# Adding a norm's shifts by a one-row product in the PSUM bank, in place of an add on VectorE

## The chip, the cores and the metric

The kernel runs on one core of a Trainium2 chip. The metric is the device time of one execution in microseconds (us); "before" is the median of three runs. Five engines work side by side and meet at semaphores: TensorE (PE in the profile, its weight loads PEld), VectorE (DVE), ScalarE (ACT), GpSimd (POOL) and the queue engine SyncE (SP), which issues DMAs.

## The reference

Two transformer-like layers are applied to x of shape 4 x 2048 x 256, in f32. Each layer derives six rows of 256 values per batch from a condition (shift, scale and gate, twice), and uses them around two blocks:

```python
mod = (_silu(L1_c) @ L1_wmod).reshape(L1_c.shape[0], 6, 1, -1)
sa, ca, ga, sb, cb, gb = (mod[:, 0], mod[:, 1], mod[:, 2], mod[:, 3], mod[:, 4], mod[:, 5])
...
h = _layernorm(x, axis=-1) * (1 + ca) + sa
x = x + ga * _L1_attn_ref(h, L1_attn_A_log, L1_attn_B, L1_attn_C, L1_attn_D)
h = _layernorm(x, axis=-1) * (1 + cb) + sb
x = x + gb * _L1_ffn_ref(h, L1_ffn_W_r, L1_ffn_W_k, L1_ffn_W_v, L1_ffn_mu_r, L1_ffn_mu_k)
```

Layer 0 is a linear attention and a mixture of 48 experts. Layer 1 is a state-space filter along the sequence (a long convolution per channel) and a gated feed-forward net. The change concerns the first norm of layer 1, `_layernorm(x) * (1 + ca) + sa`, which feeds the filter.

## The kernel before

The four stages run one after the other: `attention`, `experts`, `ssm` and `mix`. The stage `ssm` begins with the norm. The sequence of 8192 tokens (4 batches of 2048) is cut into 16 blocks of 512 tokens; a block is a tile of 128 partitions x 4 x 256 channels (`NT` = 4, `NB` = 4 blocks for each batch).

For each block n the norm does this:

- `see(n)`: the block is loaded by a DMA on SyncE's queue (L1260; the first waits until the experts' last scatters into `acc` have landed), and VectorE takes the statistics of its four parts (L1267 and L1268).
- `affine(mv, name, eng)` (L178): mean and variance become a bias and a scale per token. Inside it `rsqrt` (L155) makes four preparing operations on VectorE and three Newton steps of four operations each (L171 to L174). Without `eng` the Newton steps run on GpSimd. Blocks 0 and 1 have a call each, named n4, with `nc.vector`; from block 2 on one call, named n8, serves a pair of blocks and runs on GpSimd.
- `normal(n)`: ScalarE writes the normalized block `xh`, one activation for each part (L1274).
- `turn(n)`: VectorE multiplies `xh` by the scales `cb` (L1280) and adds the shifts `sb` (L1281). Both rows are held on all 128 partitions, loaded by a broadcasting DMA (`row`, L138). Then TensorE multiplies by a constant matrix that reverses the order of the 128 tokens (L1285), two products of 128 x 128 by 128 x 512 into two PSUM banks.
- `evict(n)`: ScalarE copies the two banks into `hch`, with channels ahead of tokens (L1292).

There are four banks (`pn`, bufs=4), so two blocks can be in them, and three tiles `xh`. The order on VectorE and ScalarE is pinned to the order of the program (`in_order`): in the loop over pairs, ScalarE normalizes blocks n-2 and n-1, then copies block n-3 out; VectorE takes the statistics of blocks n and n+1 and their bias and scale, then turns n-2 and n-1; ScalarE copies n-2 out between. The order on TensorE is chosen by the scheduler.

After the norm, the filter works on groups of 32 channels: products with the taps (L1374, 128 contraction rows), block states (L1360), and products with the carried states (L1380, 16 contraction rows). They use `hch` of all blocks, so they begin when the norm is done. The last stage, `mix`, calls `affine` with `nc.vector` for its block 0 and on GpSimd for the others.

Of the kernel before, what the change touches and what calls it, by code (L numbers as in the profile page):

```python
# [9 lines left out]
F32 = mybir.dt.float32  # L10
# [4 lines left out]
ALU = mybir.AluOpType  # L15
# [4 lines left out]
P = 128  # L20
B, N, D = 4, 2048, 256
# [4 lines left out]
NT = 4  # L26
# [19 lines left out]
class Net:  # L46
# [105 lines left out]
        nc.vector.scalar_tensor_tensor(out, sign, 1.0, mag, ALU.subtract, ALU.mult)  # L152


    def rsqrt(self, mv, name, eng=None):  # L155

        nc = self.nc
        n = mv.shape[1]
        eng = eng or nc.gpsimd

        def col(t):
            return self.stat.tile([P, n], F32, name=f"{name}{t}")

        v, nh, y = col("v"), col("h"), col("y")
        nc.vector.tensor_scalar(v, mv[:, :, 1], EPS_LN, None, ALU.add)
        nc.vector.tensor_scalar(nh, v, -0.5, None, ALU.mult)
        nc.vector.tensor_scalar(y.bitcast(I32), v.bitcast(I32), 1, None, ALU.logical_shift_right)
        nc.vector.tensor_scalar(y.bitcast(I32), y.bitcast(I32), -1.0, float(0x5F3759DF), ALU.mult, ALU.add)  # L168
        for i in range(3):
            t, z = col(f"t{i}"), col(f"z{i}")  # L170
            eng.tensor_tensor(t, y, y, ALU.mult)  # L171
            eng.tensor_tensor(t, t, nh, ALU.mult)
            eng.tensor_scalar(t, t, 1.5, None, ALU.add)
            eng.tensor_tensor(z, y, t, ALU.mult)  # L174
            y = z
        return y

    def affine(self, mv, name, eng=None):  # L178

        nm, nb = (self.stat.tile([P, mv.shape[1]], F32, name=f"{name}{t}") for t in ("nm", "nb"))  # L180
        self.nc.vector.tensor_scalar(nm, mv[:, :, 0], -1.0, None, ALU.mult)
        rs = self.rsqrt(mv, name, eng)
        (eng or self.nc.gpsimd).tensor_tensor(nb, nm, rs, ALU.mult)
        return nb, rs

# [1051 lines left out]
    def ssm(self):  # L1237


        nc, tc, a, cst = self.nc, self.tc, self.a, self.cst  # L1240
        carry = cst[:, C_CARRY:C_CARRY + T // P]
        NBLK = B * NB
        with ExitStack() as own:
# [6 lines left out]
            ga = self.row(gp, 1, 2, "ga1")  # L1250
            with tc.tile_pool(name="sn", bufs=2) as sn, tc.tile_pool(name="pn", bufs=4, space=PSUM) as pn:
                cb = self.row(sn, 1, 1, "cb1")
                sb = self.row(sn, 1, 0, "sb1")
                av = self.acc.rearrange("(g t p) c -> g p t c", p=P, t=NT)
                sh = [P, NT, D]
                stat, xhs, turned = {}, {}, {}

                def see(n, mv):

                    nc.sync.dma_start(out=self.xs[n], in_=av[n])  # L1260
                    if n == 0:
                        for was in self.added:
                            tc.add_manual_dep(nc.cur_bb.bb.instructions[-1], was.name, mybir.DependencyInfo(
                                mybir.DependencyClass.Sync, mybir.DependencyReason.DATA), reason="all is added")
                    for i in range(NT):
                        st = self.stat.tile([P, 6], F32, name="bnst", bufs=4)
                        nc.vector.bn_stats(st, self.xs[n][:, i, :])  # L1267
                        nc.vector.bn_aggr(mv[:, i, :], st)  # L1268

                def normal(n):  # L1270
                    nb, rs = stat.pop(n)
                    xh = xhs[n] = sn.tile(sh, F32, name="xh", bufs=3)
                    for i in range(NT):
                        nc.scalar.activation(xh[:, i, :], self.xs[n][:, i, :], AF.Identity, bias=nb[:, i:i + 1],  # L1274
                                             scale=rs[:, i:i + 1])

                def turn(n):

                    b, xh = n // NB, xhs.pop(n)
                    nc.vector.tensor_tensor(xh, xh, cb[:, b, :].unsqueeze(1).to_broadcast(sh), ALU.mult)  # L1280
                    nc.vector.tensor_tensor(xh, xh, sb[:, b, :].unsqueeze(1).to_broadcast(sh), ALU.add)  # L1281
                    turned[n] = []
                    for i in range(0, NT, 2):
                        ps = pn.tile([P, 2, D], F32, name="turn")
                        nc.tensor.matmul(ps, cst[:, C_TURN:C_TURN + P], xh[:, i:i + 2, :], start=True, stop=True)  # L1285
                        turned[n].append(ps)

                def evict(n):
                    b, g = divmod(n, NB)
                    for i, ps in enumerate(turned.pop(n)):  # L1290
                        k = 1 + g * NT + 2 * i
                        nc.scalar.copy(h[:, :, b, k:k + 2].rearrange("p c t -> p t c"), ps)  # L1292

                with self.in_order(mybir.EngineType.DVE, mybir.EngineType.Activation):
                    for n in range(2):
                        mv = self.stat.tile([P, NT, 2], F32, name="mv4")
                        see(n, mv)
                        if n:
                            turn(0)
                        stat[n] = self.affine(mv, "n4", nc.vector)  # L1300
                        normal(n)
                    evict(0)
                    for n in range(2, NBLK, 2):
                        if n > 2:
                            normal(n - 2)
                            normal(n - 1)
                            evict(n - 3)
                        mv = self.stat.tile([P, 2 * NT, 2], F32, name="mv8")
                        see(n, mv[:, 0:NT, :])
                        see(n + 1, mv[:, NT:, :])  # L1310
                        nb, rs = self.affine(mv, "n8")
                        for j in range(2):
                            r = slice(j * NT, (j + 1) * NT)
                            stat[n + j] = nb[:, r], rs[:, r]
                        if n > 2:
                            turn(n - 2)
                            evict(n - 2)
                        turn(n - 1)
                    for n in range(NBLK - 2, NBLK):
                        normal(n)  # L1320
                    evict(NBLK - 3)
                    for n in range(NBLK - 2, NBLK):
                        turn(n)
                        evict(n)
# [9 lines left out]
            for G in range(D // CG):  # L1334
                c0 = G * CG
                taps = []
                for q in range(4):


                    t = tap[:, (4 * G + q) % NTAP, :, :]  # L1340
# [6 lines left out]
                for j in range(4):  # L1347
                    nc.sync.dma_start(out=gt[32 * j:32 * j + NST, :, :],
                                      in_=self.gk[c0 + j:c0 + CG:4, :, :].rearrange("g s l -> s g l"))
# [3 lines left out]
                    out=rt, in_=a["A_row"][c0 * NST:(c0 + CG + 1) * NST].partition_broadcast(P))  # L1353
                nc.scalar.activation(rt, rt, AF.Exp, scale=cst[:, C_BACK:C_BACK + 1])
                nc.vector.tensor_scalar(rt, rt, cst[:, C_BACK + 1:C_BACK + 2], None, ALU.mult)
                ps = pst.tile([P, NG, B, NCH], F32, name="st")
# [13 lines left out]
                for j in range(4):  # L1370
                    for g in range(NG):
                        c = 4 * g + j
                        for o in halves:
                            nc.tensor.matmul(ys[j][o, g, :, :], taps[c // 8][:, c % 8, o], h[:, c0 + c, :, 1:NCH + 1],  # L1374
                                             start=g == 0, stop=False, skip_group_check=True)
                for g in range(NG):
                    for j in range(4):
                        r = slice(32 * j, 32 * j + NST)
                        for o in halves:
                            nc.tensor.matmul(ys[j][o, g, :, :], gt[r, g, o], st[r, g, :, :],  # L1380
                                             start=False, stop=g == NG - 1, skip_group_check=True)
# [257 lines left out]
```

## Time and profile before

| | |
|---|---|
| median of three runs | 1844.8 us (1840.78 to 1850.27) |
| profiled execution, its own time | 1854.75 us |
| span of the profiled execution | 1852.9 us |
| mean granted TensorE clock | 0.909 |
| busy: PE, DVE, ACT, POOL | 1597.8, 1120.8, 771.0, 573.8 us |
| the norm's first statistics start | 1435.36 us of the span |
| the norm's last copy starts | 1528.9 us |
| operations of L1281 (add of the shifts) | 16, 1225 ns each |
| records of L1285 (the turns) | 64, mean 947 ns |

Times inside the span are read from its start. A group line names the line of the kernel, the engine, the operation, the tiles (output <- inputs), their shapes and the count; then the group's busy time and the mean of one; then how long the engine was idle just before, and what ended that. A line of the view by windows has a stretch of time, its length, busy time and count of each engine, the granted clock of TensorE as a share of full speed, the busy share of the DMA engines and GB/s; where it is asked for the instructions of one line, only the engines that this line uses are given. In the timeline, a line has the start, the duration, the engine and the operation.

### The profile page before, as it was taken

What the parts mean: (1) busy time and instruction counts of PE and PEld (TensorE: products, weight loads), DVE (VectorE), ACT (ScalarE), POOL (GpSimd) and SP (SyncE); (2) the same over time, 40 slices, a digit from 0 to 9 for tenths busy, and PEclk for the clock granted to TensorE, in tenths of its full rate; (3) what the DMA queues carried; (4) which work ended last, traced back from release to release, by engine and by line L of the source; (5) the groups of instructions that cost most, each with busy time, mean ns of one, the idle gap of its engine ahead of it and who ended that gap; (6) DMA issues with size and microseconds to landing.
All of it is one profiled execution on the core that took longest, in us unless ns stands there. A gap on an engine that the chain in (4) does not pass through costs nothing. (4 is left out here: it accounts for less than half of the span.)

```text
span 1852.9 us, 42083 instructions
## 1 busy us (share of the span) xinstructions
PE 1597.8 (86%) x17071; PEld 1135.5 (61%) x17071; DVE 1120.8 (60%) x3364; ACT 771.0 (42%) x1528; POOL 573.8 (31%) x922
## 2 busy tenths in 40 slices
PE   6999998999899998944599999899996467959998
PEld 3576566656665675521377777677775126847776
DVE  4745665467546642568577777643442976478874
ACT  1354334433443443334355455433332582217653
POOL 1110111011101000117466666767774350013220
PEclk9999998999899997865699999999998667769999
DMA  5400123012301210241377888788885607420111
GB/s 164 138 14 13 61 81 100 14 60 74 106 3 49 63 39 13 73 164 52 114 207 208 227 230 218 220 222 246 238 232 137 185 1 126 97 58 35 46 46 57
DMA packets 145409, 205.23 MB, mean 111 GB/s; under 512 B 13704, under 2 KB 121064, under 8 KB 139072
## 3 DMA queue, kind: packets, MB, share of 16 engines
q1 hardware_dynamic: 114920, 146.23, 25.6%
q0 software_dynamic: 26240, 50.61, 11.8%
q10 hardware_dynamic: 4056, 5.70, 1.1%
q8 instruction: 134, 2.20, 0.5%
q14 instruction: 59, 0.48, 0.1%
HBM read 149.27 MB, written 51.69 MB: 108 GB/s over the span
## 5 line engine op out<-in xcount | busy, mean ns | idle before, releaser
L869 PE MATMUL h<-xT,w 128*128 128x256 f32 x1536 | 365.9, 386 | 2.8 <-issue 1.3
L869 PEld LDWEIGHTS h<-xT,w 128*128 128x128 f32 x1536 | 281.8, 191 | 47.4 <-issue 9.8
L872 ACT ACTIVATE hg<-h,b 128x256 f32<-128x256 f32 x384 | 160.3, 468 | 214.5 <-PE h L869 173.1
L903 POOL DMA_INDIRECT acc<-ys,tok x96 | 153.5, 1599 | 40.7 <-issue 21.9
L411 DVE TENSOR_REDUCE mk<-quad 128x4 f32<-128x512 f32 x128 | 79.5, 684 | 100.5 <-PE quad L358 100.5
L803 POOL DMA_INDIRECT xrow<-hd,tok x96 | 94.8, 988 | 113.8 <-DVE take L1049 39.5
L612 ACT ACTIVATE e<-quad 128x512 f32<-128x512 f32 x128 | 66.2, 602 | 139.5 <-PE quad L608 139.4
L171 POOL TENSOR_TENSOR nat<-nay 128x4 f32<-128x4 f32 x16 | 5.9, 371 | 355.6 <-DVE nay L168 355.6
L1010 ACT ACTIVATE work<-work,cand 128x576 f32<-128x576 f32 (+1 forms) x93 | 68.0, 731 | 111.3 <-DVE cand L1051 83.4
L786 POOL DMA_INDIRECT rows<-tab,ridx x96 | 102.2, 1064 | 32.9 <-issue 28.9
L171 POOL TENSOR_TENSOR nbt<-nby 128x4 f32<-128x4 f32 x15 | 5.0, 331 | 320.5 <-DVE nby L168 320.5
L1285 PE MATMUL turn<-xh,cst 128*128 128x512 f32 x64 | 50.0, 947 | 57.8 <-DVE xh L1281 28.9
L887 DVE TENSOR_SCALAR yT<-y,b 128x256 f32<-128x256 f32 x96 | 41.8, 476 | 92.3 <-PE y L880 92.3
L880 PE MATMUL y<-hg,w 128*64 128x256 f32 x768 | 93.5, 385 | 0.0
L511 ACT ACTIVATE e<-quad 128x512 f32<-128x512 f32 x128 | 66.1, 602 | 52.1 <-PE quad L504 52.1
L416 DVE TENSOR_REDUCE qm<-quad 128x8 f32<-128x512 f32 x128 | 79.0, 678 | 13.1 <-PE quad L358 13.0
L880 PEld LDWEIGHTS y<-hg,w 128*64 128x64 f32 x768 | 50.9, 136 | 36.7 <-issue 15.9
L1285 PEld LDWEIGHTS turn<-xh,cst 128*128 128x128 f32 x64 | 18.4, 305 | 88.9 <-issue 55.9
L1009 DVE TENSOR_SCALAR_CACHE_REDUCE work<-work,cand 128x448 f32<-128x448 f32 (+1 forms) x93 | 68.3, 735 | 3.4
L604 PE MATMUL quad<-qT,pj 32*128 32x512 f32 x256 | 60.0, 685 | 8.9 <-ACT e L612 8.9
L397 PE MATMUL mm<-hT,Wk 128*128 128x512 f32 x128 | 63.1, 628 | 4.7 <-ACT hT L384 4.6
L1374 PE MATMUL y<-hch,tap 128*64 128x64 f32 x1024 | 57.6, 271 | 9.5 <-issue 5.9
(348 smaller groups left out, 3510.9 us busy)
## 6 DMA issues: line engine op xcount, KB each, us to landing
w<-in_W_dram SPq DMA_DIRECT2D x48, 1024.0 KB
w<-in_W_dram SPq DMA_DIRECT2D x48, 256.0 KB
xb<-in_x_dram SPq DMA_DIRECT2D x16, 512.0 KB
xr<-in_x_dram SPq DMA_DIRECT2D x16, 512.0 KB
hd<-mod SPq DMA_DIRECT2D x16, 512.0 KB
acc<-xr SPq DMA_DIRECT2D x16, 512.0 KB
hd<-h SPq DMA_DIRECT2D x16, 512.0 KB
x<-acc SPq DMA_DIRECT2D x16, 512.0 KB
```

Of the source, the lines that this page charges most:

```text
L411: largest(kb, i, lambda c, ps: nc.vector.tensor_reduce(mk[:, g, i // 2, c, :, :], ps.rearrange("p i m h j -> p m h i j"), AX.XY, ALU.max))
L416: largest(qT, i, lambda c, ps: nc.vector.tensor_reduce(qm[:, i:i + 2, 0, :, c, :], ps, AX.X, ALU.max))
L612: nc.scalar.activation(e[c], ps[c], AF.Exp)
L786: nc.gpsimd.indirect_dma_start(out=both, out_offset=None, in_=tab[e // NER][:, :], in_offset=bass.IndirectOffsetOnAxis(ap=ridx[:, sh, e:e ...
L803: nc.gpsimd.indirect_dma_start(out=row, out_offset=None, in_=hd[:, :], in_offset=bass.IndirectOffsetOnAxis(ap=tok[:, sh, e:e + 1], axis=0))
L869: nc.tensor.matmul(ps[:, mo, :], w1[:, s, kc, mo * P:(mo + 1) * P], xT[:, kc, :], start=kc == 0, stop=kc == KC - 1)
L872: nc.scalar.activation(hg[:, s, mo, :], ps[:, mo, :], AF.Gelu, bias=b1[:, e, s, mo:mo + 1])
L880: nc.tensor.matmul(ps[i * KO:(i + 1) * KO, s2, :], w2[:, 2 * s2 + i, mo, :], hg[:, 2 * s2 + i, mo, :], start=mo == 0, stop=mo == KC - 1)
L903: nc.gpsimd.indirect_dma_start(out=acc[:, :], out_offset=bass.IndirectOffsetOnAxis(ap=tok[:, sh, e:e + 1], axis=0), in_=ys, in_offset=None ...
L1009: nc.vector.tensor_scalar(njunk, z[:, 0:ND], cand, None, ALU.is_ge, ALU.add, accum_out=cnt[:, 0:1])
L1010: nc.scalar.activation(sjunk, z[:, ND:RT], AF.Sign, bias=cand, scale=-1.0, accum_out=cnt[:, 1:2])
L1285: nc.tensor.matmul(ps, cst[:, C_TURN:C_TURN + P], xh[:, i:i + 2, :], start=True, stop=True)
```

## The change

In `turn`, the add of the shifts on VectorE is gone. The two banks of a block are instead opened by a product of a row of ones (1 x 128) with the shifts of the batch (1 x 256, read twice), which writes the shifts into all 128 rows; the reversing products are accumulated on top. The shifts are loaded to one partition and no longer broadcast to 128. In `rsqrt`, the last two operations of a Newton step become one where the steps run on VectorE and the caller is `affine`, which is so in three calls: blocks 0 and 1 of this stage and block 0 of `mix`.

```diff
-    def rsqrt(self, mv, name, eng=None):
+    def rsqrt(self, mv, name, eng=None, fused=False):
...
-            eng.tensor_scalar(t, t, 1.5, None, ALU.add)
-            eng.tensor_tensor(z, y, t, ALU.mult)
+            if eng is nc.vector and fused:
+                eng.scalar_tensor_tensor(z, t, 1.5, y, ALU.add, ALU.mult)
+            else:
+                eng.tensor_scalar(t, t, 1.5, None, ALU.add)
+                eng.tensor_tensor(z, y, t, ALU.mult)
...
-        rs = self.rsqrt(mv, name, eng)
+        rs = self.rsqrt(mv, name, eng, True)
...
-                sb = self.row(sn, 1, 0, "sb1")
+                sb = sn.tile([1, B, D], F32, name="sb1", bufs=1)
+                nc.sync.dma_start(out=sb, in_=self.rowd[1:2, :, 0:D])
...
-                    nc.vector.tensor_tensor(xh, xh, sb[:, b, :].unsqueeze(1).to_broadcast(sh), ALU.add)
-                    turned[n] = []
-                    for i in range(0, NT, 2):
-                        ps = pn.tile([P, 2, D], F32, name="turn")
-                        nc.tensor.matmul(ps, cst[:, C_TURN:C_TURN + P], xh[:, i:i + 2, :], start=True, stop=True)
-                        turned[n].append(ps)
+                    turned[n] = [pn.tile([P, 2, D], F32, name="turn") for i in range(0, NT, 2)]
+                    for ps in turned[n]:
+                        nc.tensor.matmul(ps, self.ones[0:1, :], sb[:, b, :].unsqueeze(1).to_broadcast([1, 2, D]),
+                                         start=True, stop=False)
+                    for i, ps in enumerate(turned[n]):
+                        nc.tensor.matmul(ps, cst[:, C_TURN:C_TURN + P], xh[:, 2 * i:2 * i + 2, :], start=False, stop=True)
```

## The prediction

> **What bounds the kernel now.** I read the groups of the stretch in which layer 1's norm runs (1435 to 1530 us of the span) first, then busy time by period, then the timeline, and last the granted TensorE clock, window by window. The groups give what the change touches:
>
> ```profile
> L1285 PE MATMUL turn<-xh,cst 128*128 128x512 f32 x64 | 50.0, 947 | 57.8 <-DVE xh L1281 28.9 <-DVE n4v L165 24.9 <-ACT hch L1292 4.0
> L1292 ACT COPY hch<-turn 128x512 f32<-128x512 f32 x32 | 32.6, 1090 | 8.5 <-PE turn L1285 8.5
> L1281 DVE TENSOR_TENSOR xh<-xh,sb 128x1024 f32<-128x1024 f32 x16 | 19.6, 1225 | 0.6
> L1280 DVE TENSOR_TENSOR xh<-xh,cb 128x1024 f32<-128x1024 f32 x16 | 19.6, 1224 | 5.5 <-ACT xh L1274 5.5
> ```
>
> The 32 products of L1285 are 64 records: each f32 product is two passes. They wait for VectorE (L1281), while VectorE's adds are preceded by almost no idle time (0.6 us). Two periods of the loop, each a pair of blocks:
>
> ```profile
> core 0: us, PE busy (x) PEld busy (x) DVE busy (x) ACT busy (x) POOL busy (x), PEclk, DMA share, GB/s
> 1491.43:1501.31 9.88, 6.37 (x8) 2.48 (x8) 9.36 (x26) 8.09 (x13) 6.41 (x13) 0.65 0.00 1
> 1501.31:1511.19 9.88, 6.55 (x8) 2.52 (x8) 9.36 (x26) 8.10 (x13) 6.41 (x13) 0.65 0.00 0
> ```
>
> VectorE is busy 9.36 of 9.88 us, the rest being gaps between its instructions, so it sets the period. ScalarE has 1.8 us to spare and TensorE about 3.4, at a mean clock of only 0.65. The timeline shows VectorE's four big operations of one period, and the weight loads of the passes in a slow and a fast stretch:
>
> ```profile
> 1491.43 1.23 DVE L1280 TENSOR_TENSOR xh<-xh,cb 128x1024 f32<-128x1024 f32 x1
> 1492.69 1.22 DVE L1281 TENSOR_TENSOR xh<-xh,sb 128x1024 f32<-128x1024 f32 x1
> 1493.84 1.22 DVE L1280 TENSOR_TENSOR xh<-xh,cb 128x1024 f32<-128x1024 f32 x1
> 1495.09 1.23 DVE L1281 TENSOR_TENSOR xh<-xh,sb 128x1024 f32<-128x1024 f32 x1
> ...
> 1497.61 0.34 PEld L1285 LDWEIGHTS turn<-xh,cst 128*128 128x128 f32 x1 [0.52 <-issue]
> 1498.46 0.34 PEld L1285 LDWEIGHTS turn<-xh,cst 128*128 128x128 f32 x1 [0.52 <-issue]
> ...
> 1527.38 0.19 PEld L1285 LDWEIGHTS turn<-xh,cst 128*128 128x128 f32 x1 [0.24 <-issue]
> 1527.81 0.19 PEld L1285 LDWEIGHTS turn<-xh,cst 128*128 128x128 f32 x1 [0.24 <-issue]
> ```
>
> A pass of 512 columns takes 0.853 us (1498.46 less 1497.61) at clock 0.5 and 0.43 us at clock 1.0. The last view is the layer's next stage, where products of 16 contraction rows (L1380) and of 128 rows (L1374) run with equal column counts. Four whole-engine windows, then the share of L1380 in the first of them and of L1374 in the third:
>
> ```profile
> 1618.88:1622.29 3.41, 3.41 (x130) 3.34 (x130) 2.21 (x3) 0.62 (x1) 0.00 (x0) 1.00 1.18 148
> 1622.29:1625.71 3.42, 2.19 (x31) 2.00 (x33) 3.35 (x5) 0.44 (x1) 0.00 (x0) 0.51 0.25 33
> 1625.71:1629.12 3.41, 3.41 (x65) 3.41 (x63) 2.34 (x3) 0.18 (x1) 0.00 (x0) 0.50 0.27 80
> 1629.12:1632.53 3.41, 3.41 (x120) 3.34 (x120) 0.71 (x2) 1.23 (x2) 0.00 (x0) 0.99 0.71 173
> ...
> 1618.88:1622.29 3.41, 3.40 (x128) 3.26 (x128) 1.00 1.18 148
> 1625.71:1629.12 3.41, 3.41 (x65) 3.41 (x63) 0.50 0.27 80
> ```
>
> The clock changes in steps of 3.41 us. A window filled with L1380, 16 rows, 3.40 of 3.41 us busy at clock 1.00, is followed by 0.51. A window filled with L1374, 128 rows, at 0.50 is followed by 0.99. So work with few contraction rows does not hold the clock here, and the change adds products with one row.
>
> **What it removes.** Sixteen adds on VectorE, 1.225 us each: 2.47 us of a period (9.88 to 7.41). Four of GpSimd's Newton operations are stretched to 1.1 us today, each beside one of the four big VectorE operations; two are left. Three calls of the Newton chain run on VectorE (blocks 0 and 1 of this stage, block 0 of the last); in each, three operations go. The chain advances 0.2 us an operation (1438.76, 1438.97, 1439.16), so 0.6 us a call. The n8 chains are on GpSimd and keep their form. Two calls are before the first pair (1.2 us), and the third, in front of 1655.34, is on the path: 0.6 us. The shifts' load shrinks from 512 KB to 4 KB. It stood among three broadcasts that moved about 300 GB/s at 1423 to 1430 us, beside the last scatter (issued by 1426.64, awaited until 1430.96): between 0 and 1.75 us, 512 KB at that rate. I take 0.7, since the scatter needs about 3 us in any case.
>
> **What it adds.** Thirty-two products of one row by 512 columns, 64 passes. No row has this form. From above the price is L1285's pass, equal in columns: 0.853 us slow, 0.43 fast. From below it is L604, 32 rows by 512 columns, 60.0 us for 256 passes, 0.234 each, where four row strips overlap. Successive one-row products share one strip, and the products of 128 rows need the whole array, so I take L1285's price. A gain is excluded: this is added work.
>
> In the built order the one-row products of blocks 0 and 1 come ahead of everything, in time in which TensorE has nothing to do: free. From then on they stand between the turns: block 2's before turn 1, block 3's before turns 2 and 3, then each block's before its own turn; twice (blocks 7 and 11) the first of the two stands before the preceding block's turn. Each waits until ScalarE has emptied its bank, and the next turn is queued behind it; ScalarE's copies wait for that turn, and behind them the normalizations that VectorE's multiplies need. A period then has 16 passes: 13.65 us at 0.5, 6.9 at full clock. ScalarE's 8.1 us is between the two, VectorE's 7.41 too. Which limit comes next is thus a matter of the clock alone.
>
> **The sum for a slow TensorE.** Block 3's first one-row product waits for ScalarE's copy of block 1. The scales of blocks 2 and 3 come 2.4 us sooner (1.2 from the chains, 1.2 from block 0's add) and 0.9 more from one unstretched GpSimd operation. ScalarE's normalization of them so moves from 1459.7 to 1456.4, lasts 4.0, and the first copy is out at 1461.4. From there 13 blocks of one-row passes (52) and 14 of turns (56) remain: 108 x 0.853 = 92.1 us, ending 1553.5. Today the last pass ends at 1528.7 (VectorE's next operation, which awaits it, starts at 1528.87). That is 24.8 us later if no window is fast. A fast window does eight passes in place of four and gives 3.41 us back. What makes one: a slow window with about 2.7 us of turn passes (1513.14 to 1516.56, started 1513.83) was followed by slow ones, one with 3.26 us (from 1523.53 to 1526.79) by fast ones. So a slow window must be about nine tenths turn passes. A turn of four passes is 3.41 us, and between turns stand 3.41 us of one-row passes, so a window must match a turn within 0.4 us either way: 0.8 of 6.83, 0.12 a window. Turns 2 and 3 stand together, 6.8 us, which gives one for certain. Of some 23 windows that is 1 + 0.12 x 22 = 3.6, or 12.4 us. Left: 24.8 - 12.4 = 12.4; less 0.7 for the load and 0.6 for the last stage: +11.1 us.
>
> The Trainium skill, "TensorE: Matmul & The Clock Gate", Part 1 (the HAM clock gate), says that about 3.4 us of sustained activity frees the clock and tells of no dependence on rows; the same page's table under "Why this matters for your kernels" says that a single product with K=32 takes as long as one with K=128. By the first the one-row products would hold the clock and the sum would be the first rival's; by the second they cost a full pass, which speaks against this change. L1380's window disagrees with the first for 16 rows.
>
> **Base.** The profiled execution took 1854.75 us, its span 1852.9; the median of the three runs is 1844.8 (1840.78 to 1850.27). The difference carries over: 1844.8 + 11.1 = 1855.9. About 0.5%, 9.2 us, is what a measurement of this kernel can tell from no change. The likeliest case's own range is one to six fast windows: 24.8 - 3.4 - 1.3 = +20 to 24.8 - 20.5 - 1.3 = +3, so 1848 to 1865.
>
> **Rivals.** First, the one-row products hold the clock. TensorE needs 6.9 us a period, and ScalarE becomes the bound: eight normalizations 4.04 and four copies 4.1, 8.1 to 8.2. Five periods x (9.88 - 8.2) = 8.4, plus 0.6 and 0.7, less some slow windows at the start: -9 us, 1836. It decides once a period's passes take under 9.9 us, a mean clock over about 0.69. For it: 108 passes without gaps are the most continuous TensorE work that this stage has had. Against it: L1380's window. Chance 0.16.
>
> Second, the phase of the windows is lucky: one locks onto the turns. A window at full clock that holds 1.3 us or more of turns stays fast (turn passes up to about 1470.0 in the window from 1468.8 kept the next one at 1.0), while TensorE alternates between the clocks. With seven to eight fast windows the sum is 24.8 - 25.6 - 1.3 = about -2 us, 1843: no change. For it: windows of 3.41 us and turns of 3.41 us have the same length, so a match repeats. Against it: nine tenths are needed to begin. Chance 0.24. The remaining 0.60 is the forecast.
>
> That the change does less than it says is counted: the shorter Newton step reaches three calls only, 1.8 us in all.
>
> **Chances and range.** Faster by over 0.5%: half of the first rival, 0.08. Slower by over 0.5%: 0.50 of the forecast's 0.60 (four fast windows or fewer) and 0.04 of the second's, 0.54. Within: 0.38. The range runs from the first rival's 1836 to the forecast with one fast window, 1865, and a microsecond: 1836 to 1866; half of the first rival is left out.
>
> **What would show it.** Right: the turn stage's mean clock stays under 0.65, VectorE idles before its multiply, waiting for ScalarE, ScalarE's copies wait for TensorE, periods are 11 to 13.6 us, and the last turn ends near 1540. Wrong: a clock over 0.8 in the periods, periods near 8.2 us with ScalarE full, or one-row passes well under 0.43 us.

## The result and the profile after

The changed kernel takes 1857.3 us, median of 18 runs (1839.37 to 1866.16), beside 1847.61 us for 18 runs of before. One of those runs, at 2155.13 us, stands apart from the other 17 (1836.44 to 1855.16) and is left out of the ratio. The ratio is 1.0044, with a 95% interval from 1.0026 to 1.0063: about 8 us slower. That is under the 0.5% that the prediction called telling, while the interval reaches beyond it. The profiled execution took 1849.38 us, one of the shorter ones (span 1847.6, mean clock 0.913).

The groups of the changed norm, by line and form, from 1430 to 1545 us of the span; they answer to the four groups shown of before:

```profile
L1290 PE MATMUL turn<-xh,cst 128*128 128x512 f32 x64 | 40.9, 776 | 7.6 <-DVE xh L1284 7.6
L1287 PE MATMUL turn<-sb,ones 1*128 1x512 f32 x56 | 33.2, 712 | 9.8 <-ACT hch L1296 9.8
L1296 ACT COPY hch<-turn 128x512 f32<-128x512 f32 x32 | 31.7, 1093 | 11.8 <-PE turn L1290 11.8
L1284 DVE TENSOR_TENSOR xh<-xh,cb 128x1024 f32<-128x1024 f32 x16 | 19.6, 1226 | 21.3 <-ACT xh L1278 21.1
```

The waits have turned as the prediction said. VectorE's multiply (L1284) now has 21.3 us of idle time ahead of it (5.5 before), nearly all of it waiting for ScalarE. ScalarE's copies wait 11.8 us for the turns (8.5 before), and the one-row products (L1287, 712 ns each, about as long as a turn's pass) wait for those copies. That is a circle through TensorE and ScalarE; VectorE has left it.

Now the clock. Its record changes only at steps of 3.41 us, here at 1480.83 and 1494.48 among others, and the windows below lie on these steps. The first two are filled by one-row passes of blocks 0 and 1, with nothing else on TensorE; the others are from the middle of the norm. Behind them come three of the windows once more, with the turns (L1290) alone:

```profile
1422.79:1426.21 3.42, 3.42 (x5) 1.34 (x5) 0.00 (x0) 0.00 (x0) 2.88 (x2) 0.50 0.35 55
1426.21:1429.62 3.41, 3.41 (x5) 0.87 (x3) 0.84 (x3) 0.00 (x0) 0.16 (x1) 0.50 0.96 327
1484.24:1487.65 3.41, 3.41 (x9) 1.31 (x8) 2.34 (x2) 3.41 (x7) 3.01 (x6) 1.00 0.00 0
1487.65:1491.07 3.42, 3.42 (x9) 1.31 (x8) 3.22 (x14) 3.42 (x6) 0.18 (x1) 1.00 0.01 2
1491.07:1494.48 3.41, 2.77 (x6) 0.69 (x5) 3.04 (x11) 3.41 (x8) 1.47 (x2) 1.00 0.00 0
1494.48:1497.89 3.41, 2.79 (x3) 1.00 (x4) 3.24 (x11) 1.47 (x2) 2.67 (x10) 0.50 0.00 0
...
1484.24:1487.65 3.41, 1.57 (x5) 0.68 (x4) 1.00 0.00 0
1487.65:1491.07 3.42, 1.58 (x5) 0.65 (x4) 1.00 0.01 2
1491.07:1494.48 3.41, 0.86 (x2) 0.03 (x1) 1.00 0.00 0
```

Two windows filled with one-row passes leave the clock at 0.50 (its record has 0.50 until 1450.11). But windows in which one-row passes and turns alternate, with 1.57 us of turns in each, keep it at 1.00. The stretch ends behind a window with only 0.86 us of turns, although TensorE is busy for 2.77 us of it, and TensorE is back at 0.50.

The norm, from its first statistics to the filter's first tap product, took 91.9 us (94.8 before). The filter stage, from there to the start of its last addition to x, took 123.0 us (118.5 before), though no line of it was changed. These two stages together explain only +1.6 us in these two executions, and no more than +5.0 in the other two profiles of the changed kernel (e1 and e12 below), so part of the 8 us has no place in a profile. The experiments compare whole kernels.

### The profile page after: what moved, and what is told of

It reads as the page before. It is cut to its first block, busy times and chain, and to the rows that moved or that the text cites. A ratio compares the mean times of both kernels' runs of the same rounds, so it can differ in the third digit from the quotient of the medians.

```text
span 1847.6 us, 42163 instructions
## 1 busy us (share of the span) xinstructions
PE 1633.6 (88%) x17135; PEld 1149.6 (62%) x17135; DVE 1101.4 (60%) x3339; ACT 770.3 (42%) x1528; POOL 558.4 (30%) x922
## 3 DMA queue, kind: packets, MB, share of 16 engines
q0 software_dynamic: 26240, 50.61, 11.8%
## 5 line engine op out<-in xcount | busy, mean ns | idle before, releaser
L872 PEld LDWEIGHTS h<-xT,w 128*128 128x128 f32 x1536 | 282.2, 191 | 47.1 <-issue 10.8
L1378 PEld LDWEIGHTS y<-hch,tap 128*64 128x64 f32 x1024 | 53.9, 178 | 15.7 <-issue 6.3
L408 PE MATMUL mm<-Wv,hT 128*128 128x256 f32 x256 | 63.4, 390 | 0.0
```

The costliest lines, as they stand in the source:

```text
L872: nc.tensor.matmul(ps[:, mo, :], w1[:, s, kc, mo * P:(mo + 1) * P], xT[:, kc, :], start=kc == 0, stop=kc == KC - 1)
```

## The experiments

Four theories. A: products with few rows take a full pass but do not count for the clock. B: the clock is indifferent to rows, and the cost is passes, order or waits. C: the shorter Newton step or the last stage moves the time. D: the filter stage is longer because TensorE's later instructions stand 64 pass pairs (matmul and weight load) further on in its stream.

All comparisons are with before, run on the same chip beside them, in three series: e1 to e4, e5 to e8 and e9 to e12 (medians of before 1841.76, 1840.84 and 1842.89 us). "Slow" is the mean, over the runs of a kernel, of (1 - mean clock) x time: what the reduced clock withheld; "rest" is clock x time, so that the two add up to the mean time. "Norm" and "filter" are the stages above, in the one profiled execution. The row of before has the runs of the first series and the first profile; in the other two, slow and rest are 164.8 and 1678.2, 163.8 and 1678.5 us.

| kernel | median us | ratio (95%) | slow | rest | norm | filter |
|---|---|---|---|---|---|---|
| before (24 runs) | 1841.76 | 1 | 163.9 | 1678.0 | 94.8 | 118.5 |
| e1 changed kernel | 1852.54 | 1.0068 (1.0043 to 1.0092) | 166.9 | 1684.4 | 91.8 | 123.1 |
| e12 changed kernel, one run | 1854.79 | | 172.5 | 1682.3 | 96.2 | 122.1 |
| e2 128 rows | 1836.97 | 0.998 (0.9956 to 1.0004) | 149.1 | 1689.3 | 87.7 | 123.0 |
| e11 32 rows | 1842.03 | 1.0004 (0.9978 to 1.0029) | 157.7 | 1684.9 | 91.9 | 123.3 |
| e3 no shifts | 1824.92 | 0.9911 (0.9883 to 0.9938) | 153.2 | 1670.3 | 81.1 | 116.9 |
| e5 one column | 1834.46 | 0.9968 (0.9943 to 0.9992) | 159.6 | 1676.4 | 86.6 | 122.8 |
| e10 one column, all in front | 1836.73 | 0.9969 (0.9953 to 0.9985) | 156.9 | 1679.8 | 81.8 | 122.8 |
| e8 shifts behind the turn | 1848.68 | 1.0042 (1.0026 to 1.0059) | 162.9 | 1685.4 | 95.5 | 125.5 |
| e4 Newton alone | 1838.97 | 1.0001 (0.9979 to 1.0023) | 162.6 | 1678.1 | 94.5 | 119.8 |
| e6 bf16, 3 rows | 1838.08 | 0.9981 (0.9955 to 1.0008) | 159.3 | 1679.0 | 91.7 | 116.2 |
| e7 bf16, 128 rows, 3 parts | 1833.09 | 0.9952 (0.9929 to 0.9975) | 154.6 | 1678.8 | 89.1 | 116.2 |
| e9 bf16, 128 rows, 2 parts | 1828.14 | 0.9926 (0.9903 to 0.995) | 152.7 | 1675.9 | 86.3 | 117.4 |

### e1 and e12: the changed kernel again

The kernel is unchanged.

> The changed kernel once more, for a second profile at another position of the clock's windows. Theory A (the one-row products take full passes and do not count as work for the clock): 1.002 to 1.007 of the kernel before; fast windows in the norm's stage as a matter of luck, so single runs lie some 20 us apart and a run's time falls as its mean granted clock rises. Theory B (the clock does not depend on rows; the loss comes from twice the passes and from turns queued behind one-row products): the same ratio, but runs no further apart than those of the kernel before (about 10 us), and the stage's clock close to 1.0 wherever TensorE is busy without gaps.

> The changed kernel once more, for another profile: its runs spread over 1839 to 1866 us by the phase of the clock's windows against the turns. Theory A: the time goes with the norm's mean clock: 92 us at 0.81 as in the two profiles so far (1846 to 1849 us), 100 to 110 us at 0.65 to 0.7 in a run of 1856 to 1866 us. Rival (the spread is elsewhere): norm 92 us whatever the time.

Measured: 1.0068, and a single run of 1854.79 us. The seven runs of e1 lie 11 us apart (1846.2 to 1857.12), where theory A expected some 20; the 24 runs of before beside them lie 15 apart. The profile of e1, its fastest run, is like the first; that of e12, a slower execution, has a norm of 96.2 us. Four windows of e12, again on the clock's steps, with the turns (L1290) alone; all passes together keep TensorE busy through each of them (3.41 of 3.41 us):

```profile
1479.32:1482.73 3.41, 2.58 (x3) 1.18 (x4) 0.50 0.00 0
1482.73:1486.15 3.42, 1.49 (x3) 0.29 (x2) 0.50 0.00 0
1486.15:1489.56 3.41, 3.41 (x4) 0.89 (x4) 0.50 0.00 0
1489.56:1492.97 3.41, 1.57 (x5) 0.68 (x4) 1.00 0.00 0
```

TensorE is full for 10.2 us and yet at 0.50. Only the window that the turns fill is followed by 1.00. The norm of 96.2 us, at a mean clock of 0.73 (0.77 in the other two profiles), lies between the two cases of the expectation, as the time of this execution does. That is theory A's side, though the case of 100 to 110 us was not met with, and the norm is only part of the difference: of the 8.6 us between the spans of e1 and e12, 4.3 lie in the norm and 5.7 in the stages ahead of it (1.4 us are won back behind it). Over all 18 runs of the first comparison the time goes with the clock: 1839.37 us at 0.918 and 1866.16 us at 0.904, which is 150.8 and 179.2 us withheld: 28 us, as much as the 27 us between the two times. Where in the kernel they were withheld is not shown; the runs above 1855 us have no profile.

### e2 and e11: the same passes with 128 and with 32 rows

```diff
-                sb = sn.tile([1, B, D], F32, name="sb1", bufs=1)
-                nc.sync.dma_start(out=sb, in_=self.rowd[1:2, :, 0:D])
+                sb = sn.tile([128, B, D], F32, name="sb1", bufs=1)
+                nc.vector.memset(sb, 0.0)
+                nc.sync.dma_start(out=sb[0:1, :, :], in_=self.rowd[1:2, :, 0:D])
...
-                        nc.tensor.matmul(ps, self.ones[0:1, :], sb[:, b, :].unsqueeze(1).to_broadcast([1, 2, D]),
+                        nc.tensor.matmul(ps, self.ones[0:128, :], sb[:, b, :].unsqueeze(1).to_broadcast([128, 2, D]),
```

This is e2; e11 has 32 in the three places of 128.

> The shift products have 128 rows in place of one: row 0 holds the shifts, the other 127 are zeros. Same columns, same passes, same order. Theory A: the granted clock is near 1.0 in the periods, a period is 8.2 to 8.5 us (ScalarE), and the time falls to 0.994 to 0.997 of the kernel before, 10 us or more under the changed kernel. Theory B: nothing moves against the changed kernel: 1.002 to 1.007.

> The shift products have 32 rows (shifts on row 0, 31 rows of zeros) instead of 1. With 1 row the ratio was 1.0044 and 1.0068, with 128 rows 0.998. Theory A in the form of a threshold on rows (16 rows did not hold the clock in the filter stage): 32 rows behave as 1 row, mean clock in the norm about 0.81 or less, ratio 1.002 to 1.008. Theory A in the form of a share (a product counts by its rows): nearly as 1 row, 1.000 to 1.005. Rival (any non-trivial number of rows will do, or the zeros do not matter): as 128 rows, norm 88 us, clock 0.89, ratio 0.997 to 0.999.

The eight products of blocks 0 and 1 run back to back on an otherwise idle TensorE, so they are a measurement by themselves. The timeline of the changed kernel, then of the kernel with 32 rows, then with 128:

```profile
1422.54 7.16 PE L1287 MATMUL turn<-sb,ones 1*128 1x512 f32 x8 [6.45 <-DMA sb<-rowd]
```

```profile
1413.15 7.16 PE L1288 MATMUL turn<-sb,ones 32*128 32x512 f32 x8 [6.62 <-DMA sb<-rowd]
```

```profile
1413.52 6.71 PE L1288 MATMUL turn<-sb,ones 128*128 128x512 f32 x8 [6.55 <-DMA sb<-rowd]
```

And the windows around them, on the clock's steps, with 32 rows and with 128:

```profile
1413.61:1417.03 3.42, 3.42 (x5) 1.33 (x5) 0.00 (x0) 0.00 (x0) 2.71 (x2) 0.50 0.25 43
1417.03:1420.44 3.41, 3.29 (x4) 0.67 (x3) 0.95 (x4) 0.00 (x0) 0.00 (x0) 0.50 1.04 353
1420.44:1423.85 3.41, 0.00 (x0) 0.00 (x0) 2.96 (x18) 0.00 (x0) 0.00 (x0) 0.50 1.09 348
```

```profile
1416.22:1419.63 3.41, 3.41 (x6) 1.34 (x4) 0.05 (x1) 0.00 (x0) 0.95 (x1) 0.50 0.76 262
1419.63:1423.04 3.41, 0.60 (x2) 0.00 (x0) 3.06 (x16) 0.00 (x0) 0.00 (x0) 1.00 1.03 332
```

With 32 rows a full window and one with 3.29 of 3.41 us bring no clock; with 128, of which 127 are zeros, one full window brings it, in the eighth pass, and it stands at full for a window in which almost nothing is left to do. So eight passes take the same time with 1 and with 32 rows, and with neither do they raise the clock by themselves. The same shows in a clock that is up. A window from the middle of the norm and the one behind it, with 128 rows and then with 32:

```profile
1460.59:1464.00 3.41, 2.53 (x6) 0.76 (x4) 2.89 (x12) 3.38 (x7) 0.90 (x2) 1.00 0.00 0
1464.00:1467.42 3.42, 1.28 (x3) 0.68 (x4) 2.61 (x7) 3.40 (x6) 2.84 (x8) 1.00 0.01 2
```

```profile
1481.88:1485.29 3.41, 2.62 (x6) 0.66 (x4) 3.05 (x11) 3.41 (x7) 1.65 (x2) 1.00 0.00 0
1485.29:1488.71 3.42, 3.00 (x3) 1.00 (x4) 3.25 (x12) 1.29 (x2) 2.62 (x10) 0.50 0.00 0
```

TensorE is busy for 2.53 and 2.62 us; with 128 rows the clock stays, with 32 it falls (0.71 of the 2.62 us are turns). Idle time is thus not what ends the fast stretches.

In the whole kernel 128 rows take away the loss: 17.8 us less is withheld by the clock than in e1 (149.1 for 166.9), the rest of the time is not shorter (1689.3 for 1684.4), and the intervals of the ratios lie apart. That is theory A, and with 15.6 us between the medians the largest single cost of the change, although the 0.994 to 0.997 that A expected were not reached. The profiles show only part of it in its place: the norm is 4.1 us shorter than in e1 and 8.5 shorter than in e12. With 32 rows the profile is that of one row (norm 91.9 us at a mean clock of 0.77), but the interval of its ratio lies below e1's and overlaps those of 128 rows and of the first comparison. Whether 32 rows count for nothing or for a little is not settled.

### e3: the shifts left out, and e5: products of one column

In e3 the one-row products are taken out and the shifts are left out of the computation. In e5 they are there, in the same number and order and with the same waits, but with one column, so that next to nothing is streamed; the shifts are left out as well.

```diff
-                        nc.tensor.matmul(ps, self.ones[0:1, :], sb[:, b, :].unsqueeze(1).to_broadcast([1, 2, D]),
-                                         start=True, stop=False)
+                        nc.tensor.matmul(ps[:, 0, 0:1], self.ones[0:1, :], self.ones[0:1, 0:1], start=True, stop=True)
...
```

The edit shown is e5's; in both kernels the load of the shifts goes too, and the turns open their banks themselves.

> The changed kernel with the shifts left out (no add on VectorE, no one-row product; the shifts of this norm are missing from the result). Theory A and theory B alike: the price of the one-row products goes, ScalarE sets a period of 8.2 us, 0.994 to 0.997 of the kernel before, although TensorE runs slow most of the time (clock 0.6 to 0.7 in the periods). Theory C (the loss comes from the shorter Newton step or from the next stage): still 1.002 or more.

> As the run without shifts, with one-row products of a single column in place of the changed kernel's 512 columns (the shifts are missing from the result). Same number of TensorE instructions, same order, same waits for banks as in the changed kernel; only the streaming is gone. Theory A (streaming at a slow clock is the cost): the norm's stage stays at 81 to 83 us. Theory B (order and waits are the cost): it stays near the changed kernel's 92. Theory D (the filter stage behind it, 117 to 120 us without the added instructions and 123.0 to 123.1 with them, moved because TensorE's later instructions sit 64 pairs further on): the filter stage takes 123 us here too, 0.993 to 0.995 of the kernel before in all; otherwise 117 and 0.991.

e3 shows what VectorE's relief, with the shorter Newton step and without the shifts' load, is worth where nothing takes its place: 0.9911 (0.994 to 0.997 expected), some 16 us, and a norm of 81.1 us. A stretch of its steady part:

```profile
1450.00:1495.00 45.00, 26.61 (x43) 9.62 (x42) 33.12 (x106) 44.27 (x72) 22.49 (x65) 0.84 0.00 1
```

ScalarE is busy 44.27 of 45 us: it is the next limit, as the prediction's first rival had it. The change then gives all of this back, and more: 27.6 us lie between e3 and e1. e5 divides them; its norm lies between the expectations of A and B, and its filter stage is as theory D has it. Instructions that stream next to nothing cost 5.5 us in the norm (86.6 for 81.1), where ScalarE's copies now wait 5.9 us for the turns (1.0 in e3), and 5.9 us in the filter stage (122.8 for 116.9). What is left between e5 and e1, 0.0100 of the ratio or 18 us, is the streaming and the clock; the profiles show 5.2 (e1) to 9.6 us (e12) of it in the norm.

### e10: the same instructions, all in front

```diff
+                pad = pn.tile([P, 2, D], F32, name="turn")
+                for i in range(32):
+                    nc.tensor.matmul(pad[:, 0, 0:1], self.ones[0:1, :], self.ones[0:1, 0:1], start=True, stop=True)
```

added to e3, ahead of the loop; the shifts stay left out.

> The shifts are left out of the computation. Thirty-two one-row products of a single column (64 pass pairs of instructions, as many as the change adds) stand on TensorE ahead of the first turn, into a bank of their own, and wait for nothing; none stands between the turns. Theory D (the filter stage takes 123 us instead of 117 because 64 more instructions, with their weight loads, stand ahead of it in TensorE's stream): norm 81 as without shifts, filter 122 to 124, ratio about 0.994. Rival (the filter stage is longer because the norm ends at another phase of the clock or because products stand between the turns): norm 81, filter 117, ratio 0.990 to 0.992.

Norm 81.8, filter 122.8: theory D's numbers, in a kernel in which nothing stands between the turns. In all 14 profiles the filter stage takes 122.1 to 125.5 us where 64 such pairs come before it, and 116.2 to 119.8 where none do, or 32 in bf16; TensorE's order of instructions inside the stage is the same in all. The ratio, 0.9969, is above the expected 0.994; a likely reason is that the 64 passes also took 10.07 us of TensorE's queue ahead of the experts' last transposes. The whole filter stage, e3 first, then with the pad:

```profile
1502.20:1619.10 116.90, 98.29 (x2560) 90.23 (x2560) 69.19 (x85) 22.16 (x35) 0.14 (x2) 0.76 0.55 110
1511.80:1634.60 122.80, 101.82 (x2560) 92.69 (x2560) 69.33 (x86) 22.15 (x35) 0.14 (x2) 0.78 0.54 106
```

The same 2560 matmul records keep TensorE busy 3.5 us longer, at no lower clock. Two of the waits in the stage, from the view of waits, e3 first:

```profile
PEld y L1373 <- issue: 8.0, 10, 3.6
```

```profile
PEld y L1376 <- issue: 9.8, 13, 4.0
PEld y L1376 <- ACT tap L1346: 2.0, 2, 1.8
```

Columns: what waits, for what, total, times, longest. "Issue" is a stall that no semaphore explains. All such stalls of the weight loads come to 13.7 us in e3 and 15.4 with the pad, but they do not make the stage longer in general: in the three profiles of the changed kernel they come to 10.4 to 10.8 us, in that of before to 15.3, and the stage is 3.6 to 4.6 us longer all the same. What parts the two groups of profiles is TensorE's busy time in the stage (101.6 to 104.9 us behind 64 pairs, 97.2 to 99.6 otherwise) and its waits for ScalarE's copies of the taps (2.0 to 7.0 us against 0 to 1.1). That the 64 pairs in front lengthen the stage is shown; by what means they do so is not.

### e8: the shifts behind the turn

```diff
+                    for i, ps in enumerate(turned[n]):
+                        nc.tensor.matmul(ps, cst[:, C_TURN:C_TURN + P], xh[:, 2 * i:2 * i + 2, :], start=True, stop=False)
                     for ps in turned[n]:
                         nc.tensor.matmul(ps, self.ones[0:1, :], sb[:, b, :].unsqueeze(1).to_broadcast([1, 2, D]),
-                                         start=True, stop=False)
-                    for i, ps in enumerate(turned[n]):
-                        nc.tensor.matmul(ps, cst[:, C_TURN:C_TURN + P], xh[:, 2 * i:2 * i + 2, :], start=False, stop=True)
+                                         start=False, stop=True)
```

> The changed kernel with each block's one-row products behind its turns. Theory A: the passes and their rows are the same, so 1.002 to 1.009 of the kernel before, like the changed kernel. Theory B (turns queue behind one-row products that wait for banks): 5 us or more less than the changed kernel, 0.997 to 1.002.

1.0042, as theory A expected: the order inside a bank is not what costs. The passes are as many, and with as few rows.

### e4: the Newton step alone

Before, with the change's `rsqrt` and `affine` and nothing else.

> The kernel before with the shorter Newton step alone. Theories A and B: 1.8 us less, 0.999. Theory C: 1.002 or more.

1.0001 (0.9979 to 1.0023). The 1.8 us of the prediction's sum lie inside the interval; the time neither confirms nor refutes them. The profile shows the first part: blocks 2 and 3 are normalized from 23.1 us behind the first statistics (24.3 before), 1.2 us sooner, of which 0.3 is left at the end of the norm (94.5 for 94.8). Theory C's 1.002 or more was not measured, though the interval leaves room for up to 4 us; and the stretch behind the filter stage, 203.2 us before, is 202.8 to 203.2 in the three profiles of the changed kernel.

### e6, e7 and e9: bf16 parts

An f32 product is two passes, a bf16 product one (64 and 32 records for 32 products). e6 splits the shifts into three bf16 parts on three partitions, which one product adds up; e7 is e6 with 128 rows, 125 of them zero. e9 has two parts (about 16 bits of the shift), half the preparing operations, and loads the shifts first.

```diff
...
+                sf = sn.tile([2, B, D], F32, name="sf1", bufs=1)
+                nc.sync.dma_start(out=sf, in_=self.rowd[1][:, 0:D].partition_broadcast(2))
                 cb = self.row(sn, 1, 1, "cb1")
-                sb = sn.tile([1, B, D], F32, name="sb1", bufs=1)
-                nc.sync.dma_start(out=sb, in_=self.rowd[1:2, :, 0:D])
+                sba = sn.tile([P, B, D], BF16, name="sb1a", bufs=1)
+                nc.vector.memset(sba, 0.0)
+                sb, parts = sba[0:2], sn.tile([2, B, D], BF16, name="sb1b", bufs=1)
+                on = sn.tile([P, P], BF16, name="on1", bufs=1)
+                nc.vector.memset(on, 1.0)
+                with nc.allow_low_precision(reason="two parts hold 16 bits"):
+                    nc.vector.tensor_copy(parts, sf)
+                    nc.vector.tensor_tensor(sf, sf, parts, ALU.subtract)
+                    nc.vector.tensor_scalar(parts, parts, self.ident[0:2, 0:1], None, ALU.mult)
+                    nc.vector.scalar_tensor_tensor(sb, sf, self.ident[0:2, 1:2], parts, ALU.mult, ALU.add)
...
-                        nc.tensor.matmul(ps, self.ones[0:1, :], sb[:, b, :].unsqueeze(1).to_broadcast([1, 2, D]),
+                        nc.tensor.matmul(ps, on, sba[:, b, :].unsqueeze(1).to_broadcast([P, 2, D]),
```

This is e9's edit.

> The shifts as three bf16 parts (high, middle, low) on three partitions, added by a bf16 product of three rows of ones: one pass in place of two, and by the rule of one cycle a column half as long. Theory A: a period has 8 turn passes and 4 short ones, 6.8 + 1.7 us at the slow clock, 8.5, about ScalarE's 8.2 to 8.9; 0.992 to 0.997 of the kernel before, at a stage clock of 0.6 to 0.85. Theory B: between the changed kernel and the one without shifts, about 0.999.

> The same three bf16 parts in 128 rows, 125 of them zeros. Theory A: rows count for the clock, so it is higher than in the run with three rows, and the time equal or up to 5 us less: 0.990 to 0.996. Theory B: as with three rows.

> The shifts are split into two bf16 parts (high and low), held on partitions 0 and 1 of a tile of 128 rows whose other 126 rows are zero; one bf16 product of 128 rows by 512 columns per bank, one pass each. Against the variant with three parts, five operations on VectorE go from in front of the statistics and the shifts are loaded ahead of the scales. Theory A (one-row work does not count for the clock; every pass takes a full pass): the norm has 12 passes a period instead of 16, all of which count, and the preparation costs 6 us instead of 12, of which 3 or more lie before the first block arrives: first statistics to first turn 9 to 10 us (12.8 with three parts), norm about 86, filter about 116, ratio 0.990 to 0.995. Theory B (the clock does not ask for rows; only the number of passes counts): the same passes as with three rows, norm about 89 to 91, ratio 0.995 to 0.998.

Half the passes bring 0.9981 with 3 rows and 0.9952 with 128, whose intervals overlap; e6 falls short of A's range, e7 is inside it. In both, the preparation on VectorE delayed the first turn (12.7 us behind the first statistics for 8.6). e9 takes that delay back and is the best that was run: 1828.14 us, ratio 0.9926 (0.9903 to 0.995), faster than both kernels. Its groups from 1425 to 1511.3 us:

```profile
L1300 PE MATMUL turn<-xh,cst 128*128 128x512 f32 x64 | 39.7, 756 | 14.7 <-DVE xh L1294 14.7
L1306 ACT COPY hch<-turn 128x512 f32<-128x512 f32 x32 | 32.0, 1099 | 5.7 <-PE turn L1300 5.6
L1297 PE MATMUL turn<-sb1a,on 128*128 128x512 bf16 x31 | 12.8, 451 | 21.6 <-ACT hch L1306 21.6
```

In this stretch the shifts cost 12.8 us of TensorE in place of 33.2, and ScalarE's copies wait half as long for the turns (5.7 for 11.8). The filter stage takes 117.4 us, without the 5 to 6 us of the 64 pairs.

## Why the prediction was right, and where its sum was not

The predicted 1855.9 us and the measured 1857.3 agree, and the forecast of a loss is right: +11.1 us were forecast, the medians differ by 9.7 and the ratio says 8. The mechanism of the loss holds too. But that the number is so near is in good part luck: the base moved from 1844.8 to 1847.61 us, the sum behind the number holds only in its first half, and in the second, errors in both directions offset each other. The range, 1836 to 1866 us, held a gain as well as a loss.

**VectorE's share: right.** Its multiply now waits for ScalarE, the circle is the one named, and GpSimd's Newton chains fell from 43.0 to 28.7 us of busy time: 14.3 us over seven pairs of blocks, near the two stretched operations of 0.9 us a pair (12.6) that were to go (of 26 operations above 0.7 us, 16 are gone).

**Price and order of the passes: right at half clock.** A one-row pass takes 0.853 us there, which is L1285's price (the weight loads of the first eight stand 0.85 us apart, at 1424.38, 1425.23 and 1426.08). At full clock the alternation costs more than 0.43 us a pass: a turn and the one-row passes behind it, eight passes, take 3.82 us (turns start at 1482.30, 1486.12 and 1489.94), not 3.41. The Trainium skill, "TensorE: Matmul & The Clock Gate", says under "Why this matters for your kernels" that a single product with K=32 (32 contraction rows) takes as long as one with K=128. Here the eight passes take 7.16 us with 1 and with 32 rows alike, and 6.71 with 128, where the clock rose in the last of them.

**Few rows do not raise the clock: right.** The windows of the changed kernel, e11 and e2 show it without anything beside them. The rule of the same page, Part 1 (the HAM clock gate), that some 3.4 us of sustained activity frees the clock, does not hold here for products of 1 or 32 rows, with 7.16 us of them at 0.50.

**The start of the slow chain: right.** The prediction put the first copy of block 1 at 26.0 us behind the first statistics; the one-row product that waits for it loads at 1454.68, 25.94 us behind them (1428.74).

**The fast windows: wrong in number and in worth.** From there 108 passes were to take 92.1 - 12.4 = 79.7 us. They took 64.7 us in both profiles near 1848 us (1454.68 to 1519.4 in the first) and 69.0 in e12. By the text's own sign of being wrong ("a clock over 0.8 in the periods") the steady part of the norm shows it, here from 1441 to 1519 us of the first profile:

```profile
1441.00:1519.00 78.00, 68.21 (x117) 23.25 (x116) 49.60 (x158) 60.31 (x94) 28.69 (x91) 0.81 0.24 59
```

The last pass ends 90.6 us behind the first statistics, not some 105 (1540 less 1435.36). The record of the clock has 13.3 fast windows in these 64.7 us and 11.6 in e12's 69.0, where the forecast had 3.6. Two steps failed. The first is the chance that a slow window turns fast, put at 0.12: three of six slow windows did so in the first profile and three of nine in e12, one of them each time at turns 2 and 3, as the text had it for certain. Nine tenths of turn passes were not needed; 2.99, 2.94 and (in e1) 2.83 of 3.41 us were enough, 2.58 (in e12) were not. The second is the length of a fast stretch. The forecast counted each start as one window, but a stretch then lasted three windows or more on the turns' half alone, which the text had seen and had put into its second rival. Against these stands a third: a fast window did not give 3.41 us back but 2.1 (92.1 - 64.7 = 27.4 us for 13.3 windows), partly because eight passes take 3.82 us in it and TensorE stood idle for 3.6 us of the 64.7. So the second rival's course is what the profiles show for the norm, and its end, no change, is what the norm alone would have given (91.9 and 96.2 us beside 94.8); its "seven to eight" windows come to the same time as the 13.3 and 11.6 only because each was priced too high. For the runs above 1855 us, with clocks down to 0.904, the count is open.

**The stage behind it: missing.** The prediction had the filter stage unchanged. It grew by 4.5 us (123.0 for 118.5; 122.1 in e12), which e10 ties to the 64 pairs in front of it. It stands in no term of the sum and fills part of the place of the fast windows that were not allowed for; what fills the rest no profile shows.

**The gain that is given back: too small.** Where the one-row passes go, the relief of VectorE is worth 16 us (e3), not the first rival's 9. With one row that rival's dividing line, a mean clock over about 0.69, was crossed (0.77 over the norm), and yet the norm is only 2.9 us shorter than before: a mean does not tell that slow windows, in which the passes take longer than ScalarE's work, alternate with fast ones. With 128 rows the norm is 7.1 us shorter than before, near the 8.4 that the rival worked out; the filter's growth then left 0.998 of it.

**Load and Newton step.** The load was put too low. From the end of the last scatter's issue to the operation that waits for its landing, 4.4 us pass in before and in e4, which broadcast the shifts, and 2.7 to 2.9 in the three profiles of the changed kernel: 1.5 us, not 0.7, near the upper bound of 1.75. The 1.8 us of the Newton step cannot be told from nothing by the time of e4.

## What to carry to other kernels

Work moved from a full engine to an idle one has to be priced at the clock that the idle engine will have there: on TensorE, passes with few contraction rows take their full time and do not raise the clock, so zero rows that fill the array can pay, and one bf16 pass in place of two f32 passes pays more. An engine's stream is also a place: instructions added in one stage can lengthen the next, so compare stage by stage with a variant that keeps the instructions and drops their work. And where a prediction comes out right, its terms still need comparing, since some of them may have failed in opposite directions.

## What the runs showed of the hardware

Zeros count: 128 rows, 127 of them zero, raised the clock within eight passes (6.71 us), where 32 rows with 31 zeros did not in 7.16 us. A clock that is up needs less to stay up than it needs to rise: windows with 1.57 us of turns, the rest one-row passes, stayed at 1.00, while a slow window with 2.58 us of turns stayed slow and ones with 2.83 us and more turned fast. A window with 0.86 us of turns ended the fast stretch, though TensorE was busy for 2.77 us of it. And 64 pass pairs that stream almost nothing, placed in front, lengthen a later, unchanged stage by 5.9 us (122.8 for 116.9).
